# Two-layer vision block on one core: the first image's x kept in idle tiles while its weights are turned between chunks, and the last image's stores and half of its normalisations moved to other engines

## The chip, the cores and the metric

One core of one Trainium2 chip. The metric is the device time of one execution in microseconds (us); lower is better. A core has TensorE (PE; PEld is its weight load), VectorE (DVE), ScalarE (ACT), GpSimd (POOL) and SyncE (SP), each with an instruction queue that it works through in order, and 16 DMA engines that all queues share. DMAs can be issued from SP's queue and from ScalarE's, among others; the issue takes a place in that queue.

## The reference: what is computed

x has 16 images of 56 x 56 pixels and 384 channels, all float32. Two layers, each added to its input:

```python
x = x + dilated_attention(gn(x))     # layer 0
x = x + binary_conv(gn(x))           # layer 1
# gn: mean and variance per image and group of 12 channels, over all pixels
# dilated_attention: q, k, v = w_qkv @ x; three groups of 128 channels (4 heads of 32)
#   with dilations 1, 2, 3; softmax over 3 x 3 neighbours; then w_proj @ y + b_proj
# binary_conv: depthwise 3 x 3, every weight reduced to its sign
```

Since gn needs the mean and variance over a whole image, no pixel of an image can enter the attention before all of the image has been read, nor the convolution before all of its attention is done.

## The kernel before, in words

An image is cut into seven chunks of 8 rows (448 pixels, `PX`); 112 chunks in all, numbered m, with image b and chunk c. A chunk goes through three plans:

- `plan_a` (lines 354 to 396): `load` brings the chunk from DRAM with pixels on the partitions (`xin`, 672 KB, L373; for the first image two of three chunks use z's idle tiles, `xin_z`). `turn(j)` transposes 128 channels at a time on TensorE (L378), ScalarE copies them from PSUM to `xa` (L382, three buffers), VectorE takes their statistics (L383) and a DMA stores `xa` to a scratch tensor `xd` in DRAM (L385; for the first image from ScalarE's queue, else from SP's). After chunk 6 `norm` turns the statistics into mean and scale in six steps (`group_norm`, L286 to L339, ending with `mr`).
- `plan_b`: `load_x` fetches the chunk from `xd` as `xn` (L408, three buffers), ScalarE normalises it (L412), TensorE projects to k, v and q (L416), VectorE multiplies q by shifted k (L466), TensorE sums (L451), softmax, a DMA transpose of the weights (L516), spreading on TensorE (L529), times v on VectorE (L536), sums on GpSimd (L544 to L548); `load_residual` fetches x again as `xr` (L552), the output projection is added (L562, L565) and stored to `x1d` (L570).
- `plan_c`: the binary convolution. Channels of the first two groups (j = 0, 1) are loaded as `z` in four quarters of 32 channels, each with its three row shifts on 96 partitions (L634). `normalise(j)` is four ScalarE activations, one a quarter (L639), and `convolve(j)` twelve matmuls with diagonal matrices `kdiag` (L656), in the order of quarters 3, 0, 1, 2 for each of three shifts. The third group is loaded as `xg` (L670, two buffers), normalised to `zg` (L681), and its nine taps are made by ScalarE and GpSimd, or for the last image by VectorE (`taps_last`, L694). `turn(s)` transposes the result back for four blocks of 112 pixels (L724), ScalarE copies to `osb` (L726, two buffers), and SP's queue stores it (L727).

Nine planned steps lie between chunks. Each piece of work is given a step with `at(step, order, piece)`; pieces are issued in the order of step and kind, and a scheduler makes each engine's order of them. Chunk m's `plan_a` starts at step 9(m - 9), its `plan_b` at 9m, its `plan_c` at 9(m + 10): stage a, b and c of three images run at once in the middle, while the first image's stage a stands alone at the head and the last image's stage c alone at the tail. Each DMA also waits, through its shared completion counter, for the DMA eight places earlier in the program.

Ahead of the plans stands a setup (L147 to L221), with a pool of its own: `w_qkv` and `w_proj` are loaded and turned on TensorE (L166, L172; copied by ScalarE to `wqkvT` and by VectorE to `wprojT`), the bias is turned, the nine tap loads (L157, pieces of 4 bytes) are clipped and reduced to signs by VectorE (L195 to L201), and GpSimd builds `spread_f` and `eye3`, from which VectorE makes `spread` and `kdiag`. Only then do the first image's transposes come in TensorE's order.

Of the kernel before, what the change touches and what calls it, by code (L numbers as in the profile page):

```python
# [8 lines left out]
F32 = mybir.dt.float32  # L9
# [3 lines left out]
ALU = mybir.AluOpType  # L13
# [4 lines left out]
P = 128  # L18
HEADS = 4
# [16 lines left out]
def dilated_attention_then_binary_conv(  # L36
# [90 lines left out]
            )  # L127


    xin_p = ctx.enter_context(tc.tile_pool(name="xin_p", bufs=1))  # L130
    z_p = ctx.enter_context(tc.tile_pool(name="z_p", bufs=2))
    xa_p = ctx.enter_context(tc.tile_pool(name="xa_p", bufs=3))
    st_p = ctx.enter_context(tc.tile_pool(name="st_p", bufs=2))


    wqkvT = const.tile([P, NG, 3 * C], F32, name="wqkvT")
    wprojT = const.tile([P, NG, C], F32, name="wprojT")
    bias = const.tile([P, NG], F32, name="bias")
# [5 lines left out]
    ktap = const.tile([P, NTAP], F32, name="ktap")  # L144

    kdiag = const.tile([K3, 3, JG * NQ, HD], F32, name="kdiag")
    with tc.tile_pool(name="setup", bufs=1) as setup:  # L147
        wq_in = setup.tile([P, 9, C], F32, name="wq_in")
        nc.sync.dma_start(wq_in, w_qkv.rearrange("(t p) c -> p t c", p=P))
        wp_in = setup.tile([P, 3, C], F32, name="wp_in")  # L150
        nc.scalar.dma_start(wp_in, w_proj.rearrange("(t p) c -> p t c", p=P))
        b_in = setup.tile([NG, P], F32, name="b_in")
        nc.scalar.dma_start(b_in, b_proj.rearrange("(j p) -> j p", p=P))
        k_in = setup.tile([K3, 3, NG * NQ], F32, name="k_in")
        for ky in range(3):
            for kx in range(3):
                nc.scalar.dma_start(  # L157
                    k_in[ky * HD : (ky + 1) * HD, kx, :],
                    w_conv[ky, kx].rearrange("(s c) m -> c (s m)", c=HD),
                )  # L160

        for cc in range(NG):
            for t3 in range(3):
                pt = ps_mt.tile([P, 512], F32, tag="mt", name="pt_wq")
                for i in range(3):
                    nc.tensor.transpose(  # L166
                        pt[:, i * P : (i + 1) * P], wq_in[:, t3 * 3 + i, cc * P : (cc + 1) * P], ident
                    )
                nc.scalar.copy(wqkvT[:, cc, t3 * C : (t3 + 1) * C], pt[:, :C])
            pt = ps_mt.tile([P, 512], F32, tag="mt", name="pt_wp")  # L170
            for i in range(3):
                nc.tensor.transpose(pt[:, i * P : (i + 1) * P], wp_in[:, i, cc * P : (cc + 1) * P], ident)  # L172
            nc.vector.tensor_copy(wprojT[:, cc, :], pt[:, :C])

        pt = ps_mt.tile([P, 512], F32, tag="mt", name="pt_b")
        nc.tensor.transpose(pt[:, :NG], b_in, ident[:NG, :NG])
        nc.vector.tensor_copy(bias, pt[:, :NG])

        spread_f = setup.tile([P, 2, P], F32, name="spread_f")
        nc.gpsimd.memset(spread_f, 0.0)  # L180
        for rg in range(4):
            for f in range(2):
                for t in range(TERMS):
                    nc.gpsimd.affine_select(
                        out=spread_f[:, f].rearrange("r (h d) -> r h d", h=HEADS),
                        in_=spread_f[:, f].rearrange("r (h d) -> r h d", h=HEADS),
                        compare_op=ALU.not_equal, fill=1.0, base=-(32 * rg + (2 * t + f) * HEADS),
                        pattern=[[-1, HEADS], [0, HD]], channel_multiplier=1,
                    )
        nc.vector.tensor_copy(spread, spread_f)  # L190

        def binary(dst, k_raw):

            kc = setup.tile(list(k_raw.shape), F32, tag="kc", name="kc")
            nc.vector.tensor_scalar(kc, k_raw, -1.0, 1.0, op0=ALU.max, op1=ALU.min)  # L195
            kn = setup.tile(list(k_raw.shape), F32, tag="kn", name="kn")
            nc.vector.tensor_single_scalar(dst, kc, 0.0, op=ALU.is_gt)
            nc.vector.tensor_single_scalar(kn, kc, 0.0, op=ALU.is_lt)
            nc.vector.tensor_sub(dst, dst, kn)
            nc.vector.tensor_sub(dst, dst, kc)  # L200
            nc.vector.tensor_add(dst, kc, dst)  # L201

        kp = setup.tile([K3, 3, NG * NQ], F32, name="kp")
        binary(kp.rearrange("p k s -> p (k s)"), k_in.rearrange("p k s -> p (k s)"))
        kg_in = setup.tile([P, NTAP], F32, name="kg_in")
        nc.scalar.dma_start(kg_in, w_conv.rearrange("y x c m -> c (y x m)")[JG * P : (JG + 1) * P, :])
        binary(ktap, kg_in)
        eye3 = setup.tile([K3, HD], F32, name="eye3")
        nc.gpsimd.memset(eye3, 0.0)
        for ky in range(3):  # L210
            nc.gpsimd.affine_select(
                out=eye3, in_=eye3, compare_op=ALU.not_equal, fill=1.0, base=-ky * HD,
                pattern=[[-1, HD]], channel_multiplier=1,
            )
        for kx in range(3):
            nc.vector.tensor_tensor(
                kdiag[:, kx],
                kp[:, kx, : JG * NQ].unsqueeze(2).to_broadcast([K3, JG * NQ, HD]),
                eye3.unsqueeze(1).to_broadcast([K3, JG * NQ, HD]),
                ALU.mult,  # L220
            )  # L221


    dr_p = ctx.enter_context(tc.tile_pool(name="dr_p", bufs=3, space=DRAM))
    xn_p = ctx.enter_context(tc.tile_pool(name="xn_p", bufs=3))
    xr_p = ctx.enter_context(tc.tile_pool(name="xr_p", bufs=2))
# [29 lines left out]
    for s in range(2):  # L256
        t = const.tile([P, ROWS + 2, W + 2], F32, name=f"zg_{s}")
        nc.gpsimd.memset(t, 0.0)
        zg.append(t)

    def rows(ap):
        return ap.rearrange("p (r w) -> p r w", w=W)
# [90 lines left out]
    stats0, stats1 = {}, {}  # L353
    xd, x1d = {}, {}
    mr0, mr1 = {}, {}

    def plan_a(m, t0):

        b, c = divmod(m, NCH)
        had = {}  # L360

        def load():
            if c == 0:
                stats0[b] = st_p.tile([P, NG, NCH, 6], F32, tag="stats0", name="stats0")
                xd[b] = dr_p.tile([C, H * W], F32, tag="xd", name="xd")
            if b == 0 and c % 3:

                xin = z_p.tile([P, NQ * PX], F32, tag="z", name="xin_z")[:SUB, : NSUB * C]
                xin = xin.rearrange("p (s c) -> p s c", s=NSUB)
            else:  # L370
                xin = xin_p.tile([SUB, NSUB, C], F32, tag="xin", name="xin")
            had["xin"] = xin
            nc.sync.dma_start(xin, xf[b, c * PX : (c + 1) * PX, :].rearrange("(s p) c -> p s c", p=SUB))  # L373

        def turn(j):
            pt = ps_mt.tile([P, 512], F32, tag="mt", name="pt_x")
            for s in range(NSUB):
                nc.tensor.transpose(  # L378
                    pt[:, s * SUB : (s + 1) * SUB], had["xin"][:, s, j * P : (j + 1) * P], ident[:SUB, :SUB]
                )  # L380
            xa = xa_p.tile([P, PX], F32, tag="xa", name="xa")
            nc.scalar.copy(xa, pt[:, :PX])  # L382
            nc.vector.bn_stats(stats0[b][:, j, c, :], xa)  # L383
            queue = nc.scalar if b == 0 else nc.sync
            queue.dma_start(xd[b][j * P : (j + 1) * P, c * PX : (c + 1) * PX], xa)  # L385

        steps = {}

        def norm(k):
            if k == 0:  # L390
                steps["of"] = group_norm(stats0.pop(b), lambda mr: mr0.update({b: mr}))
            steps["of"][k]()

        at(t0 - 3, LOADS, load)
        for j in range(NG):
            at(t0 + 2 * j, STAGE_A, lambda j=j: turn(j))
        if c == NCH - 1:
            for k in range(6):
                at(t0 + 5 + STAT0_SLICE[k], STATISTICS, lambda k=k: norm(k))

    def plan_b(m, t0):
# [2 lines left out]
        had = {}  # L404

        def load_x():
            had["xn"] = xn = xn_p.tile([P, NG, PX], F32, tag="xn", name="xn")
            nc.sync.dma_start(xn, chunk_of(xd[b], c))  # L408

# [199 lines left out]
    def plan_c(m, t0):  # L609
# [26 lines left out]
        def normalise(j):  # L636
            z, mrz = had[f"z{j}"], mr1[b][1]
            for q in range(NQ):
                nc.scalar.activation(  # L639
                    z[:, q], z[:, q], AF.Identity, bias=mrz[:, j, q, 0:1], scale=mrz[:, j, q, 1:2]  # L640
                )
            for edge in edges(j):
                nc.gpsimd.memset(edge, 0.0)  # L643
# [75 lines left out]
        def turn(s):  # L719
# [4 lines left out]
                nc.tensor.transpose(pt[:SUB, j * P : (j + 1) * P], src[:, s * SUB : (s + 1) * SUB], ident)  # L724
            osb = o_p.tile([SUB, C], F32, tag="osb", name="osb")
            nc.scalar.copy(osb, pt[:SUB, :C])  # L726
            nc.sync.dma_start(of[b, p0 + s * SUB : p0 + (s + 1) * SUB, :], osb)  # L727

        at(t0 - 4, LOADS, load_g)
        at(t0 - 1, NORM, normalise_g)  # L730
# [15 lines left out]
    STEP = 9  # L746
    STAT0_SLICE = (0, 1, 2, 4, 5, 7)
    STAT1_SLICE = (0, 1, 2, 4, 4, 6)
    for m in range(N):
        plan_a(m, STEP * (m - 9))  # L750
        plan_b(m, STEP * m)
        plan_c(m, STEP * (m + 10))
# [31 lines left out]
```

## Time and profile before

| | |
|---|---|
| median of 3 runs | 5464.58 us (5464.06 to 5466.99) |
| profiled execution | 5464.04 us; its span from first to last instruction 5462.3 us |
| mean granted TensorE clock | 0.977 |
| VectorE, ScalarE, GpSimd busy | 76%, 44%, 77% |
| first normalisation of the first image (L412) | 73.89 us |
| mean and scale of the last image's second layer (`mr`, L339) | 5315.29 us |
| DMA moved | 827.88 MB, mean 152 GB/s |

How to read it: a row of instructions gives a line, an engine, the operation, the tile written and the tiles read. Busy time is summed within an engine; an engine's idle time is put down to what ended it ("<-"). Stages are stretches of the span, in us from its start. The clock is the share of full speed that TensorE was granted. "xn loads" and the like name a DMA by what it fills.

### The profile page before, as it was taken

What the parts mean: (1) busy time and instruction counts of PE and PEld (TensorE: products, weight loads), DVE (VectorE), ACT (ScalarE), POOL (GpSimd) and SP (SyncE); (2) the same over time, 40 slices, a digit from 0 to 9 for tenths busy, and PEclk for the clock granted to TensorE, in tenths of its full rate; (3) what the DMA queues carried; (4) which work ended last, traced back from release to release, by engine and by line L of the source; (5) the groups of instructions that cost most, each with busy time, mean ns of one, the idle gap of its engine ahead of it and who ended that gap; (6) DMA issues with size and microseconds to landing.
All of it is one profiled execution on the core that took longest, in us unless ns stands there. A gap on an engine that the chain in (4) does not pass through costs nothing. (4 is left out here: it accounts for less than half of the span.)

```text
span 5462.3 us, 76025 instructions
## 1 busy us (share of the span) xinstructions
PE 5293.4 (97%) x26901; PEld 2335.4 (43%) x26901; DVE 4157.7 (76%) x4179; ACT 2412.6 (44%) x4203; POOL 4212.5 (77%) x3041
## 2 busy tenths in 40 slices
PE   6999999999999999999999999999999999999956
PEld 4443444444444444444444444444444444444422
DVE  3887778777777777777777778777777777877843
ACT  2223444444444444444444444544444444444433
POOL 1667788788888888888888888888888888888860
PEclk8999999999999999999999999999999999999975
DMA  5433556555555555555555555555555555545435
GB/s 165 131 105 107 153 159 166 159 156 156 157 159 160 158 159 164 155 158 158 160 164 155 160 160 159 162 158 158 155 157 157 161 161 159 160 133 135 129 93 140
DMA packets 833859, 827.88 MB, mean 152 GB/s; under 512 B 381379, under 2 KB 823238, under 8 KB 833478
## 3 DMA queue, kind: packets, MB, share of 16 engines
q1 hardware_dynamic: 825280, 817.58, 55.0%
q10 hardware_dynamic: 8198, 5.43, 0.3%
q8 instruction: 213, 3.49, 0.3%
q14 instruction: 168, 1.38, 0.1%
HBM read 468.47 MB, written 231.21 MB: 128 GB/s over the span
## 5 line engine op out<-in xcount | busy, mean ns | idle before, releaser
L544 POOL TENSOR_TENSOR w<-w 128x1344 f32<-128x1344 f32 x672 | 2049.9, 3050 | 516.2 <-DVE w L536 493.1
L466 DVE TENSOR_TENSOR t<-pq,k 128x1344 f32<-128x1344 f32 x1008 | 1535.6, 1550 | 247.7 <-PE pq L416 244.6
L416 PE MATMUL pkv<-xn,wqkvT 128*128 128x448 f32 x4032 | 1671.1, 554 | 1.3 <-ACT xa L382 1.2
L536 DVE TENSOR_TENSOR w<-pb_a,v 128x1344 f32<-128x1344 f32 x1008 | 1557.3, 1545 | 141.0 <-PE pb_a L529 74.7
L416 PEld LDWEIGHTS pkv<-xn,wqkvT 128*128 128x128 f32 x4032 | 719.9, 190 | 773.6 <-issue 727.5
L562 PE MATMUL po<-y,wprojT 128*128 128x448 f32 x2016 | 839.1, 551 | 36.1 <-POOL y L548 36.1
L416 PE MATMUL pq<-xn,wqkvT 128*128 128x448 f32 x2016 | 852.5, 558 | 0.0
L709 POOL TENSOR_TENSOR m<-m 128x1344 f32<-128x1344 f32 x210 | 639.3, 3044 | 216.0 <-ACT m L703 215.9
L639 ACT ACTIVATE z<-z,mrz 96x448 f32<-96x448 f32 x896 | 617.1, 751 | 361.4 <-DMA z<-x1d 310.9
L451 PE MATMUL ps<-t,sel 128*32 128x448 f32 x6048 | 751.9, 552 | 6.0 <-DVE t L466 6.0
L703 ACT ACTIVATE m<-zg,ktap 128x448 f32<-128x448 f32 x945 | 556.2, 657 | 292.0 <-POOL m L709 287.6
L656 PE MATMUL pc<-z,kdiag 96*32 96x440 f32 (+1 forms) x5376 | 578.5, 565 | 46.1 <-ACT z L639 26.7
L562 PEld LDWEIGHTS po<-y,wprojT 128*128 128x128 f32 x2016 | 375.2, 191 | 398.3 <-issue 345.0
L565 DVE SCALAR_TENSOR_TENSOR xr<-po,bias,xr 128x448 f32<-128x448 f32 x336 | 228.6, 680 | 369.3 <-PE po L562 369.2
L416 PEld LDWEIGHTS pq<-xn,wqkvT 128*128 128x128 f32 x2016 | 355.0, 190 | 328.9 <-issue 328.9
L663 DVE TENSOR_TENSOR x<-pc,x 128x448 f32<-128x448 f32 x224 | 139.8, 624 | 386.9 <-PE pc L656 386.9
L548 POOL TENSOR_TENSOR y<-y,w 128x448 f32<-128x448 f32 x336 | 382.5, 1138 | 23.4
L529 PE MATMUL pb_a<-aT,spread 24*128 24x448 bf16 x3024 | 383.3, 359 | 11.5 <-DVE w L536 11.2
L547 POOL TENSOR_TENSOR y<-w 128x448 f32<-128x448 f32 x336 | 382.3, 1138 | 13.8
L426 ACT COPY v<-pkv 128x448 f32<-128x448 f32 x336 | 179.6, 535 | 446.6 <-PE pkv L416 436.9
L382 ACT COPY xa<-pt_x 128x448 f32<-128x448 f32 x336 | 179.0, 533 | 399.3 <-PE pt_x L378 376.8
L426 ACT COPY k<-pkv 128x448 f32<-128x448 f32 x336 | 179.1, 533 | 391.9 <-PE pkv L416 391.3
(113 smaller groups left out, 4146.8 us busy)
## 6 DMA issues: line engine op xcount, KB each, us to landing
z<-x1d SPq DMA_DIRECT2D x608, 224.0 KB, 4.4
xn<-xd SPq DMA_DIRECT2D x112, 672.0 KB, 4.6
xr<-xd SPq DMA_DIRECT2D x112, 672.0 KB, 4.3
x1d<-xr SPq DMA_DIRECT2D x112, 672.0 KB, 3.2
out_dram<-osb SPq DMA_DIRECT2D x448, 168.0 KB, 2.9
xin<-in_x_dram SPq DMA_DIRECT2D x108, 672.0 KB, 7.0
xd<-xa SPq DMA_DIRECT2D x315, 224.0 KB, 3.1
x<-x1d SPq DMA_DIRECT2D x112, 448.0 KB, 8.2
```

The costliest lines, as they stand in the source:

```text
L416: nc.tensor.matmul(dst[:, :PX], wqkvT[:, cc, o0 : o0 + P], had["xn"][:, cc, :], start=(cc == 0), stop=(cc == NG - 1))
L451: return nc.tensor.matmul(had["ps"][32 * j : 32 * j + 32, :PX], sel[:, s0 : s0 + 32], tk, start=(i == 0), stop=(p + NQ >= NG * NTAP),)
L466: nc.vector.tensor_tensor(t.rearrange("p k (r w) -> p k r w", w=W), q3, k3, ALU.mult)
L529: return nc.tensor.matmul(pb[:, kx, :PX].rearrange("p (s n) -> p s n", s=NSUB), spread[rows_of, v % 2, :], had["a"][rows_of, :, v // 8, :] ...
L536: nc.vector.tensor_tensor(w.rearrange("p k (r w) -> p k r w", w=W), pb[:, :, :PX].rearrange("p k (r w) -> p k r w", w=W), three(kv[1][g][m ...
L544: nc.gpsimd.tensor_tensor(w0, w0, w, ALU.add)
L548: nc.gpsimd.tensor_tensor(y, y, w0[:, 2], ALU.add)
L562: nc.tensor.matmul(po[:, :PX], wprojT[:, g, j * P : (j + 1) * P], had[f"y{g}"], start=(g == 0), stop=(g == NG - 1))
L639: nc.scalar.activation(z[:, q], z[:, q], AF.Identity, bias=mrz[:, j, q, 0:1], scale=mrz[:, j, q, 1:2])
L656: return nc.tensor.matmul(pcr[q * HD : (q + 1) * HD, :, lo:hi], kdiag[:, kx, j * NQ + q, :], rows(z[:, q])[:, :, lo + kx - 1 : hi + kx - 1 ...
L703: nc.scalar.activation(rows(t[:, kx]), zp[:, ky : ky + ROWS, kx : kx + W], AF.Copy, scale=ktap[:, o : o + 1])
L709: nc.gpsimd.tensor_tensor(had["m"], had["m"], t, ALU.add)
```

## The change

*First image.* The turned chunk is no longer put into `xa` and stored piece by piece. It goes into a tile of 672 KB that is idle at that time: chunks 0 to 2 into the three `xn` buffers, 3 and 4 into the two `xr` buffers, 5 and 6 into two of the `w` buffers. One DMA on ScalarE's queue stores the whole chunk to `xd`. Chunks 0 to 2 are then normalised where they lie; chunks 3 to 6 are loaded again as before. The first image's pieces get early steps of their own (`FIRST`).

*Weights.* The setup pool is gone. The raw weights are loaded on ScalarE's queue into the `t` buffers (`w_qkv`, three parts) and a `w` buffer (`w_proj`); bias and taps on SP's queue into a tile of pool `m`. `w_qkv` is turned between the first image's chunks 3, 4 and 5, `w_proj` within the first statistics, and the small weights are built with pieces planned around the first chunks. The same functions of the raw weights are computed. GpSimd's zero-fills of k, v, `ew`, `e3` and `zg` now come before the building of `spread_f`.

*Last image.* Quarters 1 and 3 of `z` are normalised on VectorE, and the stores of the result are issued from ScalarE's queue.

```diff
-        nc.sync.dma_start(wq_in, w_qkv.rearrange("(t p) c -> p t c", p=P))
...
+    def load_weights():
+        by_rows = w_qkv.rearrange("(t p) c -> p t c", p=P)
+        for k in range(NG):
+            raw["q", k] = t = t_p.tile([P, 3, PX], F32, tag="t", name="wq_in")
+            nc.scalar.dma_start(t[:, :, :C], by_rows[:, 3 * k : 3 * k + 3, :])
+        raw["p"] = t = w_p.tile([P, 3, PX], F32, tag="w", name="wp_in")
+        nc.scalar.dma_start(t[:, :, :C], w_proj.rearrange("(t p) c -> p t c", p=P))
...
+        nc.sync.dma_start(raw["b"], b_proj.rearrange("(j p) -> j p", p=P))
+        nc.sync.dma_start(raw["kg"], w_conv.rearrange("y x c m -> c (y x m)")[JG * P : (JG + 1) * P, :])
...
+    def load_taps(ky, kx):
+        k_in = raw["k"].rearrange("p (k s) -> p k s", k=3)
+        nc.sync.dma_start(
+            k_in[ky * HD : (ky + 1) * HD, kx, :], w_conv[ky, kx].rearrange("(s c) m -> c (s m)", c=HD)
+        )
...
-            xa = xa_p.tile([P, PX], F32, tag="xa", name="xa")
+            if b == 0:
+
+                if j == 0:
+                    pool, tag = ((xn_p, "xn"), (xn_p, "xn"), (xn_p, "xn"), (xr_p, "xr"), (xr_p, "xr"), (w_p, "w"),
+                                 (w_p, "w"))[c]
+                    first[c] = pool.tile([P, NG, PX], F32, tag=tag, name="x_first")
+                xa = first[c][:, j]
+            else:
+                xa = xa_p.tile([P, PX], F32, tag="xa", name="xa")
...
-            queue = nc.scalar if b == 0 else nc.sync
-            queue.dma_start(xd[b][j * P : (j + 1) * P, c * PX : (c + 1) * PX], xa)
+            if b:
+                nc.sync.dma_start(xd[b][j * P : (j + 1) * P, c * PX : (c + 1) * PX], xa)
+            elif j == NG - 1:
+                nc.scalar.dma_start(chunk_of(xd[b], c), first[c])
...
+            if m < 3:
+                had["xn"] = first[m]
+                return
...
+                if q % 2 and b == B - 1:
+                    nc.vector.tensor_scalar(
+                        z[:, q], z[:, q], mrz[:, j, q, 1:2], mrz[:, j, q, 0:1], op0=ALU.mult, op1=ALU.add
+                    )
+                    continue
...
-            nc.sync.dma_start(of[b, p0 + s * SUB : p0 + (s + 1) * SUB, :], osb)
+
+            queue = nc.sync if b < B - 1 else nc.scalar
+            queue.dma_start(of[b, p0 + s * SUB : p0 + (s + 1) * SUB, :], osb)
...
+    FIRST = -200
+    at(FIRST, LOADS, load_weights)
+    for cc in range(NG):
+        at(FIRST + 6 + 2 * cc, STAGE_C, lambda cc=cc: turn_qkv_weights(cc))
+        at(-21 + cc, STAGE_C, lambda cc=cc: turn_proj_weights(cc))
+    at(-18, LOADS, load_small_weights)
+    for o in range(NTAP):
+        at(-17 + o, LOADS, lambda o=o: load_taps(*divmod(o, 3)))
+    at(5, LOADS, small_weights)
```

More of the change, by code (lines that the diff above doesn't have):

```diff
@@ L127, in dilated_attention_then_binary_conv @@
             )
[L130 to L133, printed above, removed]
     wqkvT = const.tile([P, NG, 3 * C], F32, name="wqkvT")
@@ L146, in dilated_attention_then_binary_conv @@
     kdiag = const.tile([K3, 3, JG * NQ, HD], F32, name="kdiag")
-    with tc.tile_pool(name="setup", bufs=1) as setup:
-        wq_in = setup.tile([P, 9, C], F32, name="wq_in")
-        nc.sync.dma_start(wq_in, w_qkv.rearrange("(t p) c -> p t c", p=P))
[L150 to L221, printed above, removed]
@@ L224, in dilated_attention_then_binary_conv @@
+    xin_p = ctx.enter_context(tc.tile_pool(name="xin_p", bufs=1))
+    z_p = ctx.enter_context(tc.tile_pool(name="z_p", bufs=2))
+    xa_p = ctx.enter_context(tc.tile_pool(name="xa_p", bufs=3))
+    st_p = ctx.enter_context(tc.tile_pool(name="st_p", bufs=2))
     dr_p = ctx.enter_context(tc.tile_pool(name="dr_p", bufs=3, space=DRAM))
@@ L259, in dilated_attention_then_binary_conv, with load_small_weights, room @@
         zg.append(t)
+    raw = {}
+    def load_weights():
[5 more added lines that the diff above has]
+        nc.scalar.dma_start(t[:, :, :C], w_proj.rearrange("(t p) c -> p t c", p=P))
+    def load_small_weights():
+        raw["small"] = t = m_p.tile([P, 3, PX], F32, tag="m", name="small")
+        flat = t.rearrange("p k n -> p (k n)")
+        at_ = [0]
+        def room(parts, n):
+            at_[0] += n
+            return flat[:parts, at_[0] - n : at_[0]]
+        raw["b"] = room(NG, P)
+        raw["k"], raw["kp"] = room(K3, 3 * NG * NQ), room(K3, 3 * NG * NQ)
+        raw["kg"] = room(P, NTAP)
+        raw["eye"] = room(K3, HD)
+        raw["spread"] = room(P, 2 * P)
+        raw["clipped"], raw["less"] = room(P, 3 * NG * NQ), room(P, 3 * NG * NQ)
+        nc.sync.dma_start(raw["b"], b_proj.rearrange("(j p) -> j p", p=P))
+        nc.sync.dma_start(raw["kg"], w_conv.rearrange("y x c m -> c (y x m)")[JG * P : (JG + 1) * P, :])
@@ new lines, in load_taps, with turn_qkv_weights @@
+    def load_taps(ky, kx):
[3 more added lines that the diff above has]
+        )
+    def turn_qkv_weights(cc):
+        for t3 in range(3):
+            pt = ps_mt.tile([P, 512], F32, tag="mt", name="pt_wq")
+            for i in range(3):
+                nc.tensor.transpose(pt[:, i * P : (i + 1) * P], raw["q", t3][:, i, cc * P : (cc + 1) * P], ident)
+            nc.scalar.copy(wqkvT[:, cc, t3 * C : (t3 + 1) * C], pt[:, :C])
@@ new lines, in turn_proj_weights, with small_weights, binary @@
+    def turn_proj_weights(cc):
+        pt = ps_mt.tile([P, 512], F32, tag="mt", name="pt_wp")
+        for i in range(3):
+            nc.tensor.transpose(pt[:, i * P : (i + 1) * P], raw["p"][:, i, cc * P : (cc + 1) * P], ident)
+        nc.vector.tensor_copy(wprojT[:, cc, :], pt[:, :C])
+    def small_weights():
+        pt = ps_mt.tile([P, 512], F32, tag="mt", name="pt_b")
+        nc.tensor.transpose(pt[:, :NG], raw["b"], ident[:NG, :NG])
+        nc.vector.tensor_copy(bias, pt[:, :NG])
+        spread_f = raw["spread"].rearrange("r (f n) -> r f n", f=2)
+        nc.gpsimd.memset(spread_f, 0.0)
+        for rg in range(4):
+            for f in range(2):
+                for t in range(TERMS):
+                    halves = spread_f[:, f].rearrange("r (h d) -> r h d", h=HEADS)
+                    nc.gpsimd.affine_select(
+                        out=halves, in_=halves, compare_op=ALU.not_equal, fill=1.0,
+                        base=-(32 * rg + (2 * t + f) * HEADS),
+                        pattern=[[-1, HEADS], [0, HD]], channel_multiplier=1,
+                    )
+        nc.vector.tensor_copy(spread, spread_f)
+        def binary(dst, k_raw):
+            parts, n = k_raw.shape
+            kc, kn = raw["clipped"][:parts, :n], raw["less"][:parts, :n]
+            nc.vector.tensor_scalar(kc, k_raw, -1.0, 1.0, op0=ALU.max, op1=ALU.min)
+            nc.vector.tensor_single_scalar(dst, kc, 0.0, op=ALU.is_gt)
+            nc.vector.tensor_single_scalar(kn, kc, 0.0, op=ALU.is_lt)
+            nc.vector.tensor_sub(dst, dst, kn)
+            nc.vector.tensor_sub(dst, dst, kc)
+            nc.vector.tensor_add(dst, kc, dst)
+        binary(raw["kp"], raw["k"])
+        kp = raw["kp"].rearrange("p (k s) -> p k s", k=3)
+        binary(ktap, raw["kg"])
+        eye3 = raw["eye"]
+        nc.gpsimd.memset(eye3, 0.0)
+        for ky in range(3):
+            nc.gpsimd.affine_select(
+                out=eye3, in_=eye3, compare_op=ALU.not_equal, fill=1.0, base=-ky * HD,
+                pattern=[[-1, HD]], channel_multiplier=1,
+            )
+        for kx in range(3):
+            nc.vector.tensor_tensor(
+                kdiag[:, kx],
+                kp[:, kx, : JG * NQ].unsqueeze(2).to_broadcast([K3, JG * NQ, HD]),
+                eye3.unsqueeze(1).to_broadcast([K3, JG * NQ, HD]),
+                ALU.mult,
+            )
+        raw.clear()
@@ L355, in dilated_attention_then_binary_conv @@
     mr0, mr1 = {}, {}
+    first = {}
     def plan_a(m, t0):
@@ L392, in norm @@
             steps["of"][k]()
-        at(t0 - 3, LOADS, load)
+        at(t0 - 3 if b else FIRST + 2 * max(c - 2, 0), LOADS, load)
         for j in range(NG):
-            at(t0 + 2 * j, STAGE_A, lambda j=j: turn(j))
+            at(t0 + 2 * j if b else FIRST + 2 * c + 1, STAGE_A, lambda j=j: turn(j))
         if c == NCH - 1:
@@ L638, in normalise @@
             for q in range(NQ):
+                if q % 2 and b == B - 1:
+                    nc.vector.tensor_scalar(
+                        z[:, q], z[:, q], mrz[:, j, q, 1:2], mrz[:, j, q, 0:1], op0=ALU.mult, op1=ALU.add
+                    )
+                    continue
                 nc.scalar.activation(
```

## The prediction

> **What bounds the kernel now.** I read the page first (engine shares, then the 40 slices), then the stages of the first and last 150 us one by one, then who waits for whom in the first 80 us, the timeline there, and the chain of waits at the end.
>
> ```profile
> PE 5293.4 (97%) x26901; PEld 2335.4 (43%) x26901; DVE 4157.7 (76%) x4179; ACT 2412.6 (44%) x4203; POOL 4212.5 (77%) x3041
> ...
> PEclk8999999999999999999999999999999999999975
> ```
>
> TensorE is busy for 97% of the span; in every 200 us stage from 600 to 5200 it has the full clock. The middle is TensorE's and the change leaves each engine's order there as it is. What can move is the head, before the first projection, and the tail, after the last attention chunk.
>
> The stages of the head (columns: stage; its length; busy time of PE, PEld, DVE, ACT, POOL; granted clock; DMA share; GB/s):
>
> ```profile
> 10.00:20.00 10.00, 4.33 (x18) 3.56 (x18) 1.87 (x1) 3.49 (x6) 10.00 (x58) 1.00 0.93 199
> 20.00:30.00 10.00, 5.78 (x28) 5.44 (x29) 6.23 (x20) 2.42 (x5) 1.70 (x9) 1.00 0.00 0
> ...
> 40.00:50.00 10.00, 4.40 (x20) 3.35 (x20) 2.82 (x5) 1.96 (x4) 0.00 (x0) 0.50 1.06 362
> ```
>
> From 20 to 30 us nothing is transferred: three chunks of x lie in SBUF and wait until the weights are turned. From 40 to 50 the DMA engines are full. Who waited (us in total, times, longest):
>
> ```profile
> ACT xa L382 <- DMA xd<-xa: 21.3, 13, 4.8
> ...
> DVE kc L195 <- DMA k_in<-in_L_conv_w_dram: 18.1, 1, 18.1
> ```
>
> The kc wait holds VectorE's queue until 21.6, wprojT's copies stand behind it, and TensorE's turning waits for these (7 us). Then 13 copies wait for a store to free one of three xa buffers. The head ends so (start, length):
>
> ```profile
> 63.16 0.53 ACT L382 COPY xa<-pt_x 128x448 f32<-128x448 f32 x1 [0.47 <-DMA xd<-xa]
> ...
> 73.63 0.17 DVE L339 COPY mr<-pp 128x6 f32<-128x6 f32 x1 [2.58 <-PE pp L335]
> 73.89 0.76 ACT L412 ACTIVATE xn<-xn,mr 128x448 f32<-128x448 f32 x1 [3.50 <-DVE mr L339]
> ```
>
> Last copy of the first image at 63.69, first normalisation at 73.89: 10.2 us of statistics. One period of the tail in the chain that ended last:
>
> ```profile
> 5402.66 4.65 PE pc L656 x24
> 5407.31 1.47 PE pt_o L724 x6
> ...
> 5408.81 3.13 DMA xg<-x1d
> ...
> 5412.02 0.87 ACT zg L681
> ...
> 5419.35 2.72 ACT z L639 x4
> ...
> 5422.11 4.63 PE pc L656 x24
> ```
>
> Between zg and z lie six taps of 0.69 on VectorE, the addition of x, turning and two osb copies. First convolutions of a chunk start at 5345.06, 5364.23, 5383.76, 5402.66, 5422.11, 5440.75: 19.14 us a chunk, with TensorE at a clock of 0.5 to 0.68.
>
> **Head.** *Removed:* 21 stores of 224 KB become seven of 672 KB; the xa wait; three loads of 672 KB of xn from DRAM; all weight work ahead of the first chunk. *Moved:* in the changed program's order x is loaded first on SP, the weights on ScalarE's queue; TensorE turns three chunks, then qkv weights between chunks 3 to 5. Taps and bias go onto SP's queue: five of nine before chunk 3's load, four between chunk 5's and 6's.
>
> Bytes that must have moved before chunk 6 has landed: x 7 x 672 KB, weights 2304 KB, stores of five chunks 3360 KB, together 10.6 MB. From 30 to 62 us before moved 10.2 MB, 318 GB/s; with full engines 362. That gives 29 to 33 us; I take 31. The taps' tiny pieces cost: from 2 to 20 us 4.5 MB moved, about 12 us at 362, in 18 us of nearly full engines, so up to 6; I take 3, as part runs beside other work. With 2 us of start chunk 6 lands at 36 (30 to 40). TensorE's twelve transposes (1.01 us for four at half clock), copies and VectorE's statistics end some 2.5 us later: last copy at 38.5.
>
> Waits added. VectorE's queue has the clipping of the taps ahead of chunk 3's statistics, and the clipping waits for all nine tap loads, the last two of which wait for chunk 3's landing and the first store. Behind it stand twelve bn_stats (0.63 each) and 4 us of small work. Landing of taps took up to 9.3 us before; if the last lands at 27, VectorE catches up at 39; at 31, some 4 us later. In the statistics nine wp transposes (0.25 each at half clock) and three wprojT copies (0.55) now stand in TensorE's and VectorE's order: partly under GpSimd's work, 1.5 us on the path (0 to 3). Chunk 7's transposes stand before the last statistics matmul on TensorE, and chunk 7's load on SP now stands behind two xr loads that used to be done earlier (672 KB each, 3.8 us at 362); before it was issued at 62.10 and used at 68.06, with 4 us of GpSimd's inversion after it as cover. I take 1.3 us (0 to 5) for this and the tap wait together.
>
> First normalisation: 38.5 + 10.2 + 1.5 + 1.3 = 51.5, before 73.89: gain 22.4 (14 to 28). After it the same matmuls follow in the same order and TensorE is full from 78 us on, so the rest shifts as a whole. Spread, kdiag and bias are needed later than they come (spread is first used at 141 before); the earlier zero-fills of GpSimd lie under the loading of chunk 0; pt_b adds one matmul (0.26). The reload of chunks 3 to 6 remains, in the old place.
>
> **Tail.** For the last image z quarters 1 and 3 go to VectorE (28 operations) and 28 stores to ScalarE's queue, two after each pair of osb copies.
>
> VectorE's price: nearest rows are 0.685 (tap, two tensors read) and the CAST of spread, 0.28 for 256 elements from SBUF, while kdiag's product of two tensors takes 0.375 for the same 256. The Trainium skill, "VectorE: DVE Perf Modes", section "The perf-mode tier table", gives a single-source f32 operation from SBUF two elements a cycle, a two-tensor one a single element; the rows agree in kind. By the tap row two quarters cost 1.37, by the CAST row scaled (0.28 and 192 more elements at 1.92 per ns, 0.1) 0.38 each, 0.76. I take 0.8 (0.7 to 1.4).
>
> A store's price on ScalarE: its two-store issues in the head took 0.81 to 0.86, so 0.43 each; the longest out store on SP took 1.69. I take 0.43. A rule speaks against the move: "DMA: Bandwidth & Descriptors", section "Issuing engines are not separate DMA queues": all issuing engines share the same 16 DMA engines, so another queue saves only the sequencer's issue time. SP's stores do hold z loads behind them here (out at 5410.78, next z at 5411.68), but z waited for a load only twice (5.4 us) in this tail. By the rule the move gains nothing, by the row at most 0.3 a chunk; I take 0.
>
> The period, with pc's start as 0: pc and pt_o to 6.15 and xg's load to 9.28 as before. Meanwhile ScalarE: two osb to 6.6, two stores to 7.45, two z to 8.8; the second pc starts at 8.2, before 8.05: what the split saves (1.4), the stores and the second copy now ahead eat. zg ends at 10.2; VectorE now does five taps, not six, before x's addition: to 14.45. Then four taps to 17.25 and its two z quarters to 18.05. ScalarE after turning: osb to 16.2, stores to 17.05, first z to 17.75, second to 18.4, needed only by the fourth matmul. So the next pc starts at 18.05: 1.1 us a chunk, and what is late is VectorE's z. Five periods give 5.5; the first chunk and its follower 0.9, as mrz's twelve loads until 5323.3 stay; in the last chunk nothing repays the stores: 0.8 before its second convolution and 0.7 behind the last copies, minus 1.5. Tail: 5 (-3 to 10).
>
> **Sum.** 22.4 + 5 = 27.4. The profiled run took 5464.04 us (span 5462.3), 0.54 under the median of 5464.58; from the median: 5437.
>
> **Rivals.** *A, the wait moves* (20%): tap loads land late and chunk 7's load comes behind xr. For: tap landings up to 9.3 us, one queue. Against: chunk 3 itself lands late enough to hide much. Head 13, tail 3: 5448. *B, loading at the full rate* (15%): 362 GB/s throughout, taps hidden; head 28, tail 8: 5428. *C, slower* (4%): each of the 28 stores holds ScalarE, and z and zg behind it, for 1.69, the longest SP issue, instead of 0.43. 28 x 1.26 = 35 against the gain of 27: 5472. It decides from 0.98 us above 0.43. Against: stores on ScalarE in the head, under full engines, took 0.33 to 0.5. *D, not passed on* (6%): the crowd of xr, chunk 7 and chunk 8 loads delays the first attention chunk and the head's shift is spent by 140 us, or the tail loses; gain 5: 5459. The forecast has 55%.
>
> **Numbers.** 0.2% is 10.9 us, about what a measurement can tell from no change. Faster: forecast, A and B, 0.90; same: D, 0.06; slower: C, 0.04. The range 5424 to 5452 takes in A and B and the bounds of head and tail together.
>
> **What would show it.** In the new profile: no stage of the head without DMA; first x_first normalisation at 47 to 58 us, and TensorE full some 4 us later; no wait of copies for stores; VectorE's wait for the taps under 31 us. In the tail: periods of 17.5 to 18.5, z on VectorE at 0.35 to 0.45, stores on ScalarE at 0.33 to 0.5. The sum is wrong if the first normalisation is past 60, or if a store on ScalarE takes over 1 us.

## The result, and the profile after

The changed kernel takes 5433.89 us (median of 4 runs, 5430.67 to 5434.42) where the kernel before takes 5464.32 (4 runs, 5463.48 to 5466.99): a ratio of 0.9942, 95% interval 0.9927 to 0.9956, or 30.4 us. The forecast was 27.4. The profiled run took 5434.42, its span is 5432.7 (before 5462.3), so by spans 29.6.

The page's rows of engines and of the granted clock, after the change:

```profile
PE 5281.6 (97%) x26901; PEld 2333.5 (43%) x26901; DVE 4166.2 (77%) x4207; ACT 2394.0 (44%) x4175; POOL 4213.6 (78%) x3041
...
PEclk8999999999999999999999999999999999999977
```

TensorE has the same 26901 instructions. The 28 instructions more on VectorE and 28 fewer on ScalarE are the split z quarters, and only the end of the clock's row differs. The gain is in the two ends: the stretch between them, from the first normalisation to the last statistics, is 2.6 us longer than before, which is within its scatter (see the part on the prediction).

**Head.** I give four places of its timeline (start, length; in brackets the wait): the transposes of chunk 6, the last copies of the first image, the statistics' result, and the first normalisation.

```profile
35.55 1.34 PE L398 MATMUL pt_x<-ident,xin 112*128 112x112 f32 x12 [1.98 <-DMA xin<-in_x_dram]
...
36.62 0.97 ACT L410 COPY x_first<-pt_x 128x448 f32<-128x448 f32 x2
...
51.56 0.17 DVE L358 COPY mr<-pp 128x6 f32<-128x6 f32 x1 [0.78 <-PE pp L354]
51.76 0.76 ACT L445 ACTIVATE x_first<-x_first,mr 128x448 f32<-128x448 f32 x1 [1.64 <-DVE mr L358]
```

The last copy ends at 37.6 (before 63.7), and the first normalisation starts at 51.76 (before 73.89): 22.1 us. Two waits, of VectorE and of TensorE, in the first 62 us say what still lies between these two (`ch` is the statistics of a channel, `pm` their first matmul):

```profile
DVE small L254 <- DMA small<-in_L_conv_w_dram: 9.5, 1, 9.5
...
PE pm L311 <- DVE ch L305: 4.0, 2, 3.8
```

VectorE stood 9.5 us before the clipping of the taps, until 32.14. It was through its statistics at 41.5, 3.9 us after the last copy, and TensorE's first statistics matmul waited for it.

**Tail.** From the last statistics (mr) to the end it was 147.0 us and is 136.9. One period, in the chain that ended last (`pc` is a convolution, `pt_o` the turning back of its result, `zg` the normalised third group):

```profile
5341.30 4.39 PE pc L694 x24
5345.69 0.81 PE pt_o L762 x6
5346.52 3.23 DMA xg<-x1d
5349.77 0.86 ACT zg L719
...
5355.47 2.98 issue
5358.45 4.35 PE pc L694 x24
```

In the last 3 us, in which the chain names nothing, VectorE's final tap and its two z quarters run:

```profile
5356.82 0.69 DVE L732 SCALAR_TENSOR_TENSOR xg<-zg,ktap,m 128x448 f32<-128x448 f32 x1
5357.43 0.93 DVE L673 TENSOR_SCALAR z<-z,mrz 96x448 f32<-96x448 f32 x2
```

The quarters end at 5358.36, and the convolution starts 0.09 after them. First convolutions start at 5305.94, 5323.41, 5341.30, 5358.45, 5375.56, 5392.46 and 5410.29. Five periods of 17.4 in the mean stand against 19.14.

### The profile page after: what moved, and what is told of

It reads as the page before. It is cut to its first block, busy times and chain, and to the rows that moved or that the text cites. A ratio compares the mean times of both kernels' runs of the same rounds, so it can differ in the third digit from the quotient of the medians.

```text
span 5432.7 us, 75987 instructions
## 1 busy us (share of the span) xinstructions
PE 5281.6 (97%) x26901; PEld 2333.5 (43%) x26901; DVE 4166.2 (77%) x4207; ACT 2394.0 (44%) x4175; POOL 4213.6 (78%) x3041
## 4 chain that ended last, share of the span: by engine, by line
PE 93%; POOL 2%; DVE 2%; DMA 1%; issue 1%; ACT 1%; SPq 0%; ACTq 0%; POOLq 0%; DVEq 0%
PE pkv L449 29%; PE pq L449 15%; PE po L595 14%; PE ps L484 12%; PE pc L694 9%; PE pb_a L562 5%; PE pt_o L762 3%; PE pt_x L398 2%; PE pt_s L519 2%; POOL w L577 1%; POOL m L747 1%; DVE w L569 0%; PE pb L321 0%; DMA xg<-x1d 0%; DVE t L499 0%
## 5 line engine op out<-in xcount | busy, mean ns | idle before, releaser
L449 PE MATMUL pkv<-xn,wqkvT 128*128 128x448 f32 x3924 | 1626.3, 554 | 1.4 <-ACT xa L410 1.4
L449 PEld LDWEIGHTS pkv<-xn,wqkvT 128*128 128x128 f32 x3924 | 699.8, 189 | 753.2 <-issue 709.8
L449 PE MATMUL pq<-xn,wqkvT 128*128 128x448 f32 x1962 | 829.7, 558 | 0.0
L677 ACT ACTIVATE z<-z,mrz 96x448 f32<-96x448 f32 x868 | 598.7, 751 | 374.6 <-DMA z<-x1d 362.1
L694 PE MATMUL pc<-z,kdiag 96*32 96x440 f32 (+1 forms) x5376 | 572.4, 554 | 37.6 <-POOL z L681 17.1
L694 PEld LDWEIGHTS pc<-z,kdiag 96*32 96x32 f32 x5376 | 179.1, 112 | 371.0 <-issue 332.5
```

The costliest lines, as they stand in the source:

```text
L449: nc.tensor.matmul(dst[:, :PX], wqkvT[:, cc, o0 : o0 + P], had["xn"][:, cc, :], start=(cc == 0), stop=(cc == NG - 1))
L677: nc.scalar.activation(z[:, q], z[:, q], AF.Identity, bias=mrz[:, j, q, 0:1], scale=mrz[:, j, q, 1:2])
L694: return nc.tensor.matmul(pcr[q * HD : (q + 1) * HD, :, lo:hi], kdiag[:, kx, j * NQ + q, :], rows(z[:, q])[:, :, lo + kx - 1 : hi + kx - 1 ...
```

## The experiments

Each kernel is the changed one with the edits shown, but for the second. Medians are given with the ratio to the kernel before, measured beside it (its medians there were 5464.2 to 5465.4, so that a difference of 1 or 2 us between two medians says little). "First normalisation" and "tail" (last mr to the end) are from the profile of each.

**1. Head alone.** The two tail edits are undone.

```
-                if q % 2 and b == B - 1:
+                if False and b == B - 1:
-            queue = nc.sync if b < B - 1 else nc.scalar
+            queue = nc.sync
```

> The head of the change alone: all normalisations of z on ScalarE and all output stores on SP's queue again. My theory: the first normalisation comes at 51.8 as in the changed kernel, 22.1 us early, of which the trace shows 19.5 left at the last statistics; the tail then takes the 147 us it took before. Time 5464.6 - 19.5 = 5445, span about 5442.8. Rival: what is lost between 22.1 and 19.5 comes from the tail's part of the change (it could not, by order of time, but a second run can show whether the loss is chance): a time of 5442.5.

5442.77 us, 0.9960 (0.9946 to 0.9975): 21.4 faster than before. First normalisation 51.89, tail 146.1. The head gives some 21, and the tail's time of before comes back. This is the rival's 5442.5 and not the 5445 of the theory: most of what seemed lost between 22.1 and 19.5 is scatter of the profiled executions.

**2. Tail alone.** The kernel before, with the split and with the last image's stores on ScalarE's queue.

> The kernel before with the tail's two edits alone. My theory: the parts add up, so from the last statistics to the end 136.9 us in place of 147.0, periods of 17.1 to 17.9, TensorE's clock in them near 0.8: time 5464.6 - 10.1 = 5454.5. Rival (the forecast's 5 us is what the edits give, and the other 5 came with the head by chance of the clock): 5459.6, periods of 18.05, clock 0.5 to 0.68.

5454.97 us, 0.9984 (0.9977 to 0.9991): 9.2 faster. Tail 137.0, periods 17.0 to 18.2. The parts add up (21.4 + 9.2 against 30.4), and the tail's 10 us don't depend on the head.

**3. Stores back on SP, split kept** (the second half of the diff of 1).

> The changed kernel with the last image's output stores back on SP's queue; the normalisations stay split. My theory (moving the stores is worth nothing, the split carries the gain): within 1.5 us of the changed kernel, 5434, periods near 17.1. Rival Q (SP's queue freed of the stores lets z and xg be loaded earlier, which is the half of the tail's gain that the forecast lacked): 5 us slower than the changed kernel, 5439, periods near 18. Rival R (the stores' 0.86 us a chunk on ScalarE delay its z): up to 5 us faster, 5429.

5426.44 us (5425.06 to 5428.19), 0.9931 (0.9916 to 0.9946): 7.5 *faster* than the changed kernel; their runs don't overlap. Tail 130.7. My theory that the move is worth nothing is wrong, Q is wrong in sign, and R is right, though not where it said: periods are 17.2 in the mean, nearly those of the changed kernel. The difference is in the last chunk, from its first convolution to the end: 22.4 us in the changed kernel, 17.1 here. The last chunk's second convolution in the changed kernel, from the timeline:

```profile
5416.45 1.24 ACTq L767 DMA_DIRECT2D out_dram<-osb  x2
5417.87 1.41 ACT L677 ACTIVATE z<-z,mrz 96x448 f32<-96x448 f32 x2 [0.95 <-ACT osb L764]
5419.39 0.28 POOL L681 MEMSET z<- 32x224 f32 x1 [9.15 <-ACT z L677]
5419.72 4.43 PE L694 MATMUL pc<-z,kdiag 96*32 96x448 f32 x24 [3.31 <-POOL z L681]
```

The same place with the stores on SP:

```profile
5412.45 0.76 ACT L677 ACTIVATE z<-z,mrz 96x448 f32<-96x448 f32 x1
5413.12 0.46 ACT L764 COPY osb<-pt_o 112x384 f32<-112x384 f32 x1
5413.32 0.28 POOL L681 MEMSET z<- 32x224 f32 x1 [6.37 <-ACT z L677]
5413.65 2.44 PE L694 MATMUL pc<-z,kdiag 96*32 96x448 f32 x24 [1.33 <-POOL z L681]
```

With the stores, ScalarE copies, copies, issues two stores, and only then normalises; the edge's zero-fill and the convolution wait for that. Without them the z stand between the copies. From first to second convolution it is 9.43 us against 6.64. The second convolution itself takes 4.43 against 2.44, at a granted clock of 0.54 against 1.00: in all nine profiles with the stores on ScalarE it takes 4.1 to 4.7, in the three with the split and the stores on SP 2.44. That the longer wait before it (3.31 against 1.33) lowered the clock is not shown: in run 5's first chunk a second convolution took 4.51 after a wait of 1.26. Nor is the loss all issue time (1.24 us here): the scheduler also ordered ScalarE anew. With the stores on SP three of ScalarE's four z of the last chunk are done by 5407.60, ahead of the copies, and one is left for this place; with the stores on ScalarE two are. The runs do not take the two apart.

**4. All normalisations on ScalarE, stores there too** (the first half of the diff of 1).

> The changed kernel with all normalisations of z on ScalarE again; the stores stay on ScalarE's queue. My theory (the split carries the gain, and stores ahead of four z cost 0.86 a chunk on the path): 10 us of the tail's gain gone and up to 5 more, 5444 to 5449, periods of 19 to 20. Rival Q (the gain is SP's freed queue): 5439 or less, periods near 18.

5449.23 us, 0.9973 (0.9963 to 0.9983): 15.3 slower than the changed kernel and 6.5 slower than the head alone. Tail 153.4, periods of 19.4 in the mean. The split carries the whole gain of the tail. The moved stores lose 6 to 7.5 us with it and without it.

**5. Clipping of the taps held back.**

```
+        nc.gpsimd.tensor_tensor(raw["clipped"][:, :2], mr0[0][:, 0, :], mr0[0][:, 1, :], ALU.add)
```

> The changed kernel with the clipping of the taps held back until the first statistics are done (its scratch is first written from mr by GpSimd, one instruction more). VectorE then takes the statistics of chunks 3 to 6 right after their copies: aggregation at about 38.5 in place of 41.5. Theory 1 (VectorE's lateness is the last thing the first normalisation waits for): 3.3 us faster than the changed kernel, 5430.6. Theory 2 (chunk 7's load is just behind: its eight transposes stand ahead of the last statistics matmul and it landed at 47.8): the first normalisation moves by 0.5 only, 5433.4, and TensorE waits longer for chunk 7's load.

5431.83 us (5431.04 to 5438.53), 0.9942 (0.9927 to 0.9957). First normalisation 51.58, 0.2 earlier, as theory 2 has it. TensorE's waits of this kernel in the first 62 us have the lines:

```profile
PE pt_x L400 <- DMA xin<-in_x_dram: 10.7, 3, 4.9
...
PE pm L313 <- DVE ch L307: 1.2, 2, 1.0
```

The wait for VectorE fell from 4.0 to 1.2, and the one for x rose from 7.5 (changed kernel) to 10.7: chunk 7.

**6. The two xr loads held back as well.**

```
+            if m < 2:
+                nc.gpsimd.tensor_tensor(xr[:, 0, :2], mr0[0][:, 0, :], mr0[0][:, 1, :], ALU.add)
```

> As the one before, and the two xr loads are also held back until the first statistics are done, so that chunk 7's load goes out as soon as chunk 6 is turned, ahead of them. By theory 2 this and the one before together give what the one before does not: chunk 7 lands at about 42, first normalisation at 48.5, 3.3 us faster than the changed kernel, 5430.6. By theory 1 nothing beyond the one before.

5430.30 us, 0.9936 (0.9920 to 0.9953). First normalisation 48.77, 3.0 earlier than in the changed kernel. VectorE's late statistics and chunk 7's late load lay beside each other; both taken away give the 3 us.

No run holds back the xr loads alone. The changed kernel's trace says what to expect of it. `pp` is the last matmul of the statistics; chunk 7's transposes stand before it on TensorE, and it reads `pair`, the end of GpSimd's chain, which hangs on VectorE's statistics:

```profile
47.83 1.73 PE L398 MATMUL pt_x<-ident,xin 112*128 112x112 f32 x8 [1.83 <-DMA xin<-in_x_dram]
...
49.85 0.18 POOL L349 TENSOR_TENSOR pair<-pair 32x1 f32<-32x1 f32 x1
50.09 1.44 PE L354 MATMUL pp<-pair,gselT 32*128 32x2 f32 x6 [0.54 <-POOL pair L349]
```

The transposes end at 49.56 and `pair` at 50.03, so an earlier chunk 7 alone would have left `pp` where it is. In run 5 `pair` ends at 47.36 and `pp` waits for the transposes until 49.91. This is read from the traces, not measured.

**7. Chunks 0 to 2 loaded again.**

```
-            if m < 3:
-                had["xn"] = first[m]
-                return
```

> The changed kernel, but chunks 0 to 2 are loaded from DRAM again for their normalisation as in the kernel before, into the same buffers. Theory (bytes and queue): one reload stands on SP ahead of chunk 6's load and two more ahead of chunk 7's, 672 KB or 1.9 us each at 362 GB/s, so the first normalisation comes 3 to 6 us later, 5437 to 5440. Rival (the reload is hidden, keeping x in the tiles is worth nothing, and the head's gain is all of the weights and stores): 5434.

5437.29 us, 0.9950 (0.9935 to 0.9965): 3.4 slower than the changed kernel. First normalisation 57.52, 5.8 later; the stage from 40 to 50 us has the DMA engines full (400 GB/s, changed kernel 204). Not reloading is worth 3 to 6 us.

**8. Stores in 21 pieces from three xa buffers, reload too.**

```
-                xa = first[c][:, j]
+            xa = xa_p.tile([P, PX], F32, tag="xa", name="xa")
...
-            elif j == NG - 1:
-                nc.scalar.dma_start(chunk_of(xd[b], c), first[c])
+            queue = nc.scalar if b == 0 else nc.sync
+            queue.dma_start(xd[b][j * P : (j + 1) * P, c * PX : (c + 1) * PX], xa)
```

> The changed kernel with the first image's x stored again piece by piece from three xa buffers (21 stores of 224 KB) and all of its chunks loaded again; the weights stay turned between the chunks. Beside the run that only reloads, it shows what the wait of copies for stores is worth. Theory (the copies' wait for stores is what held the head before, the weights' order is not): copies wait again, behind VectorE's tap wait as well, the last copy of the first image lands at 45 to 50 in place of 38.6, 7 to 12 us later than with the reload alone, time 5444 to 5450. Rival (loading is bound by bytes, and these are the same): within 2 us of the run that only reloads, 5437.3.

5447.27 us, 0.9970 (0.9959 to 0.9981): 10.0 slower than the reload alone. The copies wait again, and the last of them starts at 52.3 in place of 38.6 with the reload alone:

```profile
ACT xa L402 <- DMA xd<-xa: 25.6, 13, 9.2
```

The expected 45 to 50 was passed, the time is within 5444 to 5450. Bytes are the same, so it is mainly this wait that costs; 14 more issues of 0.33 us on ScalarE, 4.6 together, are in it and were not taken apart. The step from here to the kernel before's head (5454.97 with the same tail, run 2) is 7.7 and is all that the moved weights and taps give while the pieces stay.

**9. All qkv weights turned before the first chunk.**

```
-        at(FIRST + 6 + 2 * cc, STAGE_C, lambda cc=cc: turn_qkv_weights(cc))
+        at(FIRST, LOADS, lambda cc=cc: turn_qkv_weights(cc))
```

> The changed kernel, but all 27 qkv weights are turned before the first chunk of x, as in the kernel before. Theory (the order of turning frees the x buffers early and keeps the DMA engines at work): TensorE starts chunk 0 only when the weights have landed, at about 20 in place of 7.3, chunks 3 to 5 are loaded 8 to 12 us later, there is a stage with little DMA near 20 us again, and the time is 5442 to 5446. Rival (the stores and waits taken away are the gain, the order is not): 5436 or less.

5434.41 us, 0.9943 (0.9928 to 0.9958): as the changed kernel. My theory fell. The stage from 20 to 30 us does have less DMA (0.73 against 1.02), and the last copy starts at 41.1 in place of 37.1. But the first normalisation comes at 53.2, only 1.4 later.

**10. Is the rest of that loss hidden by the waits of 5 and 6?** The edits of 5, 6 and 9 together.

> The kernel that holds back the clipping and the two xr loads, with all qkv weights turned before the first chunk. With the waits of VectorE and of chunk 7's load left in, turning the weights first cost 4.1 us at the last copy of the first image but only 1.4 at the first normalisation. Theory (those two waits hid the rest): with them away it costs about 4 at the first normalisation, 52.9 in place of 48.8, time 5434. Rival (the order is worth only 1.4 anyway): 50.2, time 5431.7.

5432.04 us, 0.9940 (0.9924 to 0.9957). First normalisation 51.68, 2.9 later than without the edit of 9: half way between theory and rival. But the last copy is only 3.1 later here (40.3 against 37.2), not 4.1, and nearly all of that reaches the first normalisation, as the theory has it. By the median it is 1.7. So the turning between the chunks is worth 3 us where nothing hides it and 1.4 in the changed kernel.

**11. A third buffer for xg in the tail** (from t's idle tiles), stores on SP.

```
+            if b < B - 1:
+                xg = xg_p.tile([P, ROWS + 2, W], F32, tag="xg", name="xg")
+            else:
+                xg = rows(t_p.tile([P, 3, PX], F32, tag="t", name="xg_t").rearrange("p k n -> p (k n)")[:, : PX + 2 * W])
```

> The changed kernel with the output stores on SP's queue again, and the last image's xg in the three idle buffers of t in place of its own two. Theory (the period of the tail is one chain: turning out frees xg, its load of 3.1 us, zg, taps, z, convolution): with the load a period ahead, the chain no longer closes and the period falls from 17 to between 11 and 14, bounded by TensorE's 10.2 and VectorE's 8.9 busy us: 5400 to 5412. Rival (another pair of buffers, z or x1, closes the same chain at once): periods of 16 or more, 5420 or more.

5417.08 us, 0.9914 (0.9899 to 0.9929): 9.4 faster than run 3. Two periods are 12.2 us, as the theory has it, then four are 15 to 16. In those the chain runs through the loads that follow on SP's queue:

```profile
5357.56 0.43 SPq L667
5358.35 5.32 DMA z<-x1d
5363.67 4.21 PE pc L694 x24
```

So xg closed the chain before, and z's load closes it next: theory and rival each hold for a part of the tail. The two short periods are no steady state either: VectorE now does more than a chunk's taps ahead of its first z, the first convolution comes 14.6 us after mr in place of 10.1 in run 3, and VectorE is busy for only 7.3 and 3.1 us of these periods, against 8.9 in a full one. The profiled execution (5413.22) is 3.9 faster than the median, so its tail of 117.4 shows more than the runs do.

**12. Runs 11, 5 and 6 together.**

> The one before, with the clipping of the taps and the two xr loads held back as well. Theory: head and tail add up, 3.4 us faster than the one before. Rival: what the head saves is lost to TensorE's clock before the last statistics (the stretch between them has varied by 2.7 us from run to run): within 1 us of the one before.

5411.98 us, 0.9907 (0.9890 to 0.9923): the fastest, 52 under the kernel before and 22 under the changed kernel. First normalisation 47.18. It is 5.1 under run 11, where the theory had 3.4 and the rival at most 1: head and tail add up.

## Why the prediction was right, and where not

**Loading (right).** Chunk 6 was to have landed at 36 and TensorE took it up at 35.55; the last copy was to end at 38.5 and ended at 37.6. No 10 us of the head are without DMA. By 35.55 us 10.4 MB had moved (292 GB/s in the mean), where the sum had 10.6.

**Tap wait and chunk 7's load (right in kind, mis-sized).** The step put 1.3 us for both. Run 6 measures 3.0 for both, run 5 shows 0.2 for the first alone. The clipping went at 32.14, a little past the 31 that the forecast allowed. The error of 1.7 was made good by the last copy, 0.9 early, and by the turned weights in the statistics: in run 6 it is 11.1 us from the last copy's end to the first normalisation, against 10.2 before, so these cost 0.9 of the 1.5 allowed. The sum, 51.5 against 51.76, is better than its terms; that is luck.

**"The rest shifts as a whole" (right, within the scatter).** In the profiles, 22.1 us at the first normalisation are 21.0 after the first 18 projections and 19.5 at the last statistics. These projections took longer in the changed kernel, but also in run 2, which has the head of before:

```profile
52.58 9.73 PE L449 MATMUL pkv<-x_first,wqkvT 128*128 128x448 f32 x18
```

```profile
74.09 9.78 PE L416 MATMUL pkv<-xn,wqkvT 128*128 128x448 f32 x18 [0.17 <-ACT xn L412]
```

In the kernel before they took 8.61, and in all fourteen profiles 8.18 (run 5) to 9.78. They start at a granted clock of 0.50 in both kernels, and it rises to 1.00 at about 78 us in the kernel before and 58 in the changed one, 3 and 5 us after their start. From first normalisation to last mr the fourteen have 5241.2 to 5244.2 us in no order of their edits: before 5241.4, run 2 with the same head 5243.9, changed 5244.0, run 5 5241.3. So the loss is not the change's. Run 1 keeps 21.4 in the median.

**Period of the tail (right in mechanism, small in size).** VectorE's z after the final tap is the limit, as said; a pair took 0.92 to 0.93 (taken 0.8), a pair of stores 0.80 to 0.90, once 1.24 (taken 0.86). (Of the rows behind the 0.8, kdiag's product takes 0.41 us, not 0.375; the view merges two that overlap.) Yet the period is 17.4 and not 18.05: the step "pc and pt_o to 6.15 as before" didn't hold, xg's load is issued 5.2 after the convolution's start, because TensorE was granted a higher clock in these periods. One period of before and one of the changed kernel (stage; length; busy time of PE, PEld, DVE, ACT, POOL; clock; DMA share; GB/s):

```profile
5345.06:5364.23 19.17, 12.48 (x61) 4.05 (x61) 7.23 (x11) 7.99 (x14) 0.00 (x0) 0.50 0.59 147
```

```profile
5341.30:5358.45 17.15, 10.18 (x60) 3.51 (x61) 8.91 (x15) 5.40 (x9) 0.00 (x0) 0.80 0.62 164
```

**Moving the stores (wrong).** The step "I take 0" for the move, with 1.5 lost in the last chunk, failed. Run 3 shows a loss of 7.5 us by the median and 6.2 in its tail, 5.3 of them in the last chunk. The price of one store was about right, its place was not. In the periods VectorE's taps cover it; in the last chunk no taps of a next chunk stand beside, and ScalarE's z, the zero-fill and the convolution, at a low clock, stand in a row behind the stores. The split was under-valued too: in run 3 the tail is 16.3 shorter than before, 11.4 of them in the six periods, for which the steps had 6.4, and 4.5 in the last chunk, for which they had nothing. So the tail's 5 is within 5 of the 10 measured only because two larger errors, of opposite sign, cancel in part: luck. The rule of the Trainium skill, "DMA: Bandwidth & Descriptors", section "Issuing engines are not separate DMA queues", spoke against the move and was right that nothing is gained; what runs 3 and 4 add is that the move cost 6 to 7.5 us on the engine that took it over, by issue time and order together.

**Rivals.** B (full rate, taps hidden) did not come: the 5433.9 lie between its 5428 and the forecast's 5437, nearer to the forecast, and the head gave 22.1, not 28. A's wait was there at 3 us, not 9. C had the right mechanism at the wrong price: a store held ScalarE for 0.32 to 0.74, not 1.69, and the loss was 7.5, not 35. D didn't come.

**Signs.** Four of those named beforehand came out just outside: the wait for the taps ended at 32.1 (named: under 31), the period is 17.4 (17.5 to 18.5), a z quarter on VectorE takes 0.50 (0.35 to 0.45), and one store took 0.74 (0.33 to 0.5; the median is 0.34).

**What the forecast didn't split.** The head's 21 us are, from the changed kernel back: 3.4 for not reloading, 10.0 for the stores that copies no longer wait for, 7.7 for the weights and taps elsewhere. The parts are taken away in this order; another order could share them out otherwise. With whole tiles kept, turning the weights between the chunks is worth 1.4 to 3 at the first normalisation (0.5 and 1.7 by the medians of runs 9 and 10).

## What to carry to other kernels

Two late arrivals that lie beside each other hide each other: taking away one shows 0.2 us (run 5), both show 3 (run 6), so follow what is just behind the wait that ends last. A move of an instruction that is free in the steady state must be priced again at the end, where its cover is gone. Where a chain closes on a buffer, one more buffer in an idle tile can still pay after the work on the chain has been made faster: 9.4 us (run 11) on top of the split's 16.3 (run 3 against run 1).

## What the runs showed of the hardware

TensorE's granted clock in the tail was higher where the periods were shorter, but their length alone doesn't set it. In the periods of before, 18.6 to 19.5 us, it was 0.50 to 0.68, with TensorE busy for 10.6 to 12.5; in the changed kernel's of 16.9 to 17.2 it was 0.80 (10.1 to 10.2 busy), in run 3's of 17.0 to 17.2 only 0.70 (9.3 to 9.4 busy), and in run 11's two of 12.3 and 12.1 it was 0.84 and 1.00. What sets it is not shown here. On the path of the changed kernel it was worth about 1 us a period: a convolution and the turning after it took 5.2 us in place of 6.1.

A z quarter on VectorE (96 x 448, f32, two scalars per partition) took 0.503 us, longer than the prediction's estimate of 0.38 and shorter than a tap's 0.685.
